# Two attention layers and two feed-forward blocks on one core: GpSimd's five transfers of a round are divided among the round's two steps

## The chip, the cores and the metric

The kernel runs on one core of a Trainium2 chip. The metric is the device time of one execution in microseconds (us); the median of three runs of the kernel before is 3321.29 us (3320.86 to 3324.8). A core has five engines that run side by side, each through its own list of instructions in order: TensorE (PE in the profile), VectorE (DVE), ScalarE (ACT), GpSimd (POOL) and SyncE (SP). Transfers by DMA are issued by SP and by POOL here, and are carried out by the core's 16 DMA engines.

## The reference

The input x has four batches of 1024 rows of 256 numbers, all in 32-bit floats. Four blocks follow one another, each added to x: attention A, a feed-forward block, attention B, and the same feed-forward block again.

```python
x = x + _L0_attn_a_ref(_layernorm(x, axis=-1), L0_attn_a_kernel, L0_attn_a_WO)
x = x + _L0_ffn_ref(_layernorm(x, axis=-1), L0_ffn_w1, L0_ffn_b1, L0_ffn_w2, L0_ffn_b2)
x = x + _L0_attn_b_ref(_layernorm(x, axis=-1), L0_attn_b_w_down_q, ...)
x = x + _L0_ffn_ref(_layernorm(x, axis=-1), L0_ffn_w1, L0_ffn_b1, L0_ffn_w2, L0_ffn_b2)
```

Both attentions have 16 heads of 64 dimensions. For every head the scores of 1024 queries against 1024 keys are put through a softmax and multiplied by the values. Attention B also rotates pairs of dimensions of its queries and keys by the position (the rope).

## The kernel before

An attention works on pairs of heads: 4 batches times 8 pairs, each in 8 **steps** of 128 queries, so 256 steps. Two steps (HB = 2) make a **round**; an attention has 128 of them. One loop, `steps_with`, lists the work of every step for every engine, and each engine keeps that order (the schedule is manual).

For step s the loop asks PE for the scores of step s+1 (L238, into PSUM), DVE for the row maxima (L249), ACT for the exponentials (L251) into a tile p, and DVE for `turn` (L271), a transpose of p in blocks of 32 by 32 into the tile T of the round. The transpose inside 32 by 32 blocks leaves 16 **squares** of 32 partitions by 1088 numbers (136 KB each) that must still go to other partitions. `send` (L288) does that: 16 transfers from T to a second tile, pT. After the second step of a round (an odd s, `part == 0`) SP is given the first 11 squares. In the step after it (an even s, `part == 1`) POOL is given the last five (POOL_DMA = 5). In the loop that call stands before `project`.

Round h of the sends is used later by `weigh(h)` on PE (L297, in step 2h+5), and by `divide(h)` on DVE (L307, the same step), which frees pT. The pools of T and pT have two buffers each. So `turn` of step 2h+4 overwrites T of round h and waits until all 16 transfers of round h have landed, and the transfers of round h+2 wait until `divide(h)` is done.

`project(h)` follows one step after `divide(h)`: PE multiplies with the output weights (L167), ACT copies the product to `got` (L320), and POOL adds it to x (L322).

POOL also issues the loads of weights in attention A (L521, L212, L214). In attention B SP issues those (L629, L212, L214), and POOL has the rope instead. In nearly every round half of a query or key tile is handled: `change` (L645) issues two transfers that swap neighbouring partitions into a tile `turned`, in an odd step; `rotate` (L650 to L652), three elementwise operations, follows at the end of the next, even, step. In some rounds POOL also adds to x a tile that ACT has just normalised (L596), for the next batch.

The lists `pieces` hold such work, by step: those of s - EARLY come between the two halves of the exponentials, those of s at the end of the step.

Of the kernel before, what the change touches and what calls it, by code (L numbers as in the profile page):

```python
# [27 lines left out]
HB = 2  # L28
# [4 lines left out]
POOL_DMA = 5  # L33
# [6 lines left out]
def hybrid_block_kernel(  # L40
# [5 lines left out]
    nc = tc.nc  # L46
# [12 lines left out]
    def group(*shape):  # L59
        last[0] ^= 1  # L60
        return ps_mm.tile([P, *shape], F32, tag=f"m{last[0]}", name="mm")
# [101 lines left out]
    def paired(out, parts, first=True, last=True):  # L163

        for i, (lhsT, rhs) in enumerate(parts):
            for j in range(2):
                nc.tensor.matmul(  # L167
                    out[ts(j, DH)], lhsT[:, ts(j, DH)], rhs[j],
                    start=(first and i == 0), stop=(last and i == len(parts) - 1),
                )  # L170
# [10 lines left out]
    def attention(prep_batch, prep_pair, wo, loader, lead):  # L181
# [22 lines left out]
        n = len(steps)  # L204
# [22 lines left out]
        sc, probs, total, T, pT, av, oT = {}, {}, {}, {}, {}, {}, {}  # L227

        def scores(s):
            g, qs = steps[s]  # L230
            qT, kT = tiles[g]["qT"], tiles[g]["kT"]
            for j in range(2):
                sc[s, j] = ps_sc.tile([P, S], F32, tag="sc", name="sc")
            for m in range(S // 512):
                for half in range(2):
                    for j in range(2):
                        rows = slice(j * DH, (j + 1) * DH)
                        nc.tensor.matmul(  # L238
                            sc[s, j][ts(half, DH), ts(m, 512)],
                            qT()[rows, ts(2 * qs + half, DH)], kT()[rows, ts(m, 512)],  # L240
                            start=True, stop=True,
                        )

        def exponentials(s, j):
            if j == 0:
                probs[s] = pp.tile([P, NK, NG, SQ], F32, tag="p", name="p")
                total[s] = small.tile([P, 2], F32, tag="total", name="total")
            nmax = small.tile([P, 1], F32, tag="nmax", name="nmax")
            nc.vector.tensor_reduce(nmax, sc[s, j], AX.X, ALU.max, negate=True)  # L249
            place = j ^ (s % HB)  # L250
            nc.scalar.activation(  # L251
                probs[s][:, :NK2, ts(j, 2), :],
                sc.pop((s, j)).rearrange("p (k c i) -> p k c i", c=2, i=SQ), AF.Exp,
                bias=nmax, accum_out=total[s][:, place : place + 1],
            )

        def invert(s):
            t = total.pop(s)
            nc.vector.reciprocal(t, t)  # L259
            nc.scalar.copy(  # L260
                probs[s][:, NK2].rearrange("p (j c) i -> p j (c i)", j=2),
                t.unsqueeze(2).to_broadcast([P, 2, DH]),
            )

        def turn(s):
            h, q = divmod(s, HB)
            if q == 0:
                T[h] = tp.tile([P, SENT], F32, tag="T", name="T").rearrange(
                    "p (c q k i) -> p c q k i", c=NG, q=HB, k=NK
                )  # L270
            nc.vector.transpose(  # L271
                T[h][:, :, q, :, :].rearrange("p c k i -> p k c i"), probs.pop(s)
            )
# [3 lines left out]
        squares = [  # L277
            ((a + 2 * i) % NG, (c + 2 * (i ^ x)) % NG)
            for x in range(2) for a in range(2) for c in range(2) for i in range(2)
        ]  # L280

        def send(h, engine, which):
            if h not in pT:
                pT[h] = ptp.tile([P, SENT], F32, tag="pT", name="pT").rearrange(
                    "p (a q k i) -> p a q k i", a=NG, q=HB, k=NK
                )
            for a, c in which:
                engine.dma_start(pT[h][ts(c, SQ), a], T[h][ts(a, SQ), c])  # L288

        def weigh(h):  # L290

            v = tiles[HB * h // NT]["v"]()
            av[h] = [group(P) for q in range(HB)]
            for k in range(NK2):
                for q in range(HB):
                    for j in range(2):
                        nc.tensor.matmul(  # L297
                            av[h][q][ts(j ^ q, DH)], v[ts(j, DH), k, :],
                            pT[h][ts(j, DH), :, q, k, :],
                            start=(k == 0), stop=(k == NK2 - 1),  # L300
                        )

        def divide(h):
            oT[h] = otp.tile([P, HB, P], F32, tag="oT", name="oT")
            R = pT.pop(h)[:, :, :, NK2, :]
            for q, sums in enumerate(av.pop(h)):
                nc.vector.tensor_tensor(  # L307
                    oT[h][:, q].rearrange("p (a i) -> p a i", i=SQ),
                    sums.rearrange("p (a i) -> p a i", i=SQ), R[:, :, q], op=ALU.mult,
                )  # L310

        def project(h):
            g, t0 = divmod(HB * h, NT)
            b, pr = pairs[g]
            po = group(HB, D)
            for t in range(HB):
                paired(po[:, t, :], [(oT[h][:, t], [wos[g][:, t]] * 2)])
            oT.pop(h)
            got = tmp.tile([P, HB, D], F32, tag="tmp", name="got")
            nc.scalar.copy(got, po)  # L320
            xd = xs[b][:, t0 : t0 + HB, :]
            nc.gpsimd.tensor_add(xd, xd, got)  # L322

        def steps_with(others):
            for k, f in others:
                pieces.setdefault(k, []).append(f)
            for s in range(-1, n + LAG + 1):
                h, part = divmod(s - LAG, HB)
                ahead = 0 <= s + 1 < n
                if 0 <= s < n:  # L330
                    invert(s)
                if ahead:
                    scores(s + 1)
                if part == 1 and 0 <= s // HB - 1 < n // HB:
                    send(s // HB - 1, nc.gpsimd, squares[len(squares) - POOL_DMA :])
                    T.pop(s // HB - 1)
                if part == 1 and 0 <= h < n // HB:
                    project(h)
                if ahead:
                    exponentials(s + 1, 0)  # L340
                for f in pieces.get(s - EARLY, ()):
                    f()
                if part == 0 and 0 <= h < n // HB:
                    weigh(h)
                if ahead:
                    exponentials(s + 1, 1)
                if 0 <= s < n:
                    turn(s)
                if part == 0 and 0 <= h < n // HB:
                    divide(h)  # L350
                if part == 0 and 0 <= s < n:
                    send(s // HB, nc.sync, squares[: len(squares) - POOL_DMA])
                for f in pieces.get(s, ()):
                    f()
# [394 lines left out]
```

## Time and profile before

The profiled execution took 3321.26 us; its span, from the first to the last instruction, is 3319.5 us, and some 1.8 us lie around it.

| what | us |
|---|---|
| median of the runs | 3321.29 |
| profiled execution | 3321.26 |
| its span | 3319.5 |
| PE busy, share of the span | 3241.7, 98% |
| DVE | 2626.0, 79% |
| ACT | 1892.7, 57% |
| POOL | 1774.2, 53% |
| attention A, stretch 60 to 1420 us: PE / DVE / POOL busy of 1360 us | 1353.7 / 1246.0 / 578.6 |
| attention B, stretch 1700 to 3066 us: PE / DVE / POOL busy of 1366 us | 1330.3 / 1259.4 / 1084.9 |

In the profile a row of the timeline gives the start, the duration, the engine, the line and the operation; a bracket at its end gives the idle time of the engine just before it and what ended it. "SPq" is SP's queue, which issues transfers; a row that stands for many of them runs from the first issue to the end of the last. The duration of a `DMA_DIRECT2D` row is the time of the issue, not of the transfer; the time to landing is given apart. The busy share of an engine is an average over the whole span, so the table gives the two attentions apart: most of the kernel's time is theirs, and they have different limits.

### The profile page before, as it was taken

Reading aid. Unit: us, or ns where it says so; the run is one execution under the profiler, and the core shown is the slowest. Engines: PE = TensorE matmul, PEld = TensorE weight load, DVE = VectorE, ACT = ScalarE, POOL = GpSimd, SP = SyncE. Lnnn points to the kernel's source line nnn. Section 1 sums busy time; section 2 is a strip of 40 time slices with the busy share of each in tenths; the row PEclk is TensorE's granted clock in tenths of the full one; section 3 lists DMA queues with packets and bytes.
Section 4 is the critical chain, followed back from the end, with each engine's and each line's share of the span. In section 5 each row is a group of like instructions: output and inputs, shape, how many; then the busy total and the mean of one; then the engine's idle time right before and its main releaser. Section 6 shows DMA issues by size and latency. Waiting matters only on the chain.

```text
span 3319.5 us, 124467 instructions
## 1 busy us (share of the span) xinstructions
PE 3241.7 (98%) x52608; PEld 2028.1 (61%) x52608; DVE 2626.0 (79%) x2898; ACT 1892.7 (57%) x3664; POOL 1774.2 (53%) x2482
## 2 busy tenths in 40 slices
PE   8999999999999999999999999999999999998999
PEld 4666666666666666666655655656556656665666
DVE  7998998899988999931069988999899989999100
ACT  5666666665666666643356665666566666665332
POOL 3444444344444444321257887888778878886100
PEclk9999999999999999999999999999999999999999
DMA  8888888888888888830049888998899889998100
GB/s 225 224 218 218 223 224 219 219 220 222 228 212 221 220 225 222 221 82 0 7 126 243 240 241 242 250 248 242 232 247 251 241 235 251 251 254 228 41 20 19
DMA packets 250825, 659.82 MB, mean 199 GB/s; under 512 B 76352, under 2 KB 105024, under 8 KB 250272
## 3 DMA queue, kind: packets, MB, share of 16 engines
q1 hardware_dynamic: 167248, 415.43, 48.0%
q0 software_dynamic: 83024, 236.44, 25.2%
q8 instruction: 418, 6.85, 0.9%
q14 instruction: 135, 1.11, 0.1%
HBM read 43.39 MB, written 4.19 MB: 14 GB/s over the span
## 4 chain that ended last, share of the span: by engine, by line
PE 70%; DVE 9%; SPq 7%; DMA 6%; issue 3%; ACT 3%; POOL 1%; DVEq 0%; ACTq 0%; POOLq 0%
PE sc L238 20%; PE mm L297 18%; PE mm L167 14%; PE mm L413 7%; SPq L288 7%; PE ph L402 6%; DVE T L271 5%; DMA pT<-T 5%; PE mm L176 4%; DVE nmax L249 3%; ACT p L251 1%; PE mm L153 1%; POOL pT L288 1%; DVE oT L307 0%; ACT gT L406 0%
## 5 line engine op out<-in xcount | busy, mean ns | idle before, releaser
L249 DVE TENSOR_REDUCE nmax<-sc 128x1 f32<-128x1024 f32 x1024 | 1202.8, 1216 | 171.1 <-PE sc L238 161.1
L251 ACT ACTIVATE p<-sc,nmax 128x1024 f32<-128x1024 f32 x1024 | 1144.0, 1117 | 329.1 <-DVE nmax L249 328.2
L271 DVE STREAM_TRANSPOSE T<-p 128x2176 f32<-128x2176 f32 x512 | 1246.7, 2435 | 62.2 <-DMA pT<-T 46.8
L288 POOL DMA_DIRECT2D pT<-T x1280 | 625.3, 496 | 1016.8 <-DVE total L259 775.9
L238 PE MATMUL sc<-kT,qT 64*64 64x512 f32 x8192 | 1109.9, 599 | 18.1 <-ACT p L251 15.3
L297 PEld LDWEIGHTS mm<-pT,v 64*64 64x64 f32 x32768 | 960.1, 133 | 159.2 <-issue 105.1
L297 PE MATMUL mm<-pT,v 64*64 64x128 f32 x32768 | 1009.4, 270 | 12.8 <-issue 11.2
L238 PEld LDWEIGHTS sc<-kT,qT 64*64 64x64 f32 x8192 | 347.4, 133 | 408.6 <-issue 276.5
L260 ACT COPY p<-total 128x128 f32<-128x128 f32 x512 | 152.8, 298 | 509.5 <-DVE total L259 503.1
L322 POOL TENSOR_TENSOR x<-x,got 128x512 f32<-128x512 f32 x256 | 330.5, 1291 | 49.4 <-ACT got L320 45.4
L420 DVE TENSOR_TENSOR x<-x,mm 128x512 f32<-128x512 f32 x32 | 21.9, 686 | 364.7 <-PE mm L413 364.7
L167 PE MATMUL mm<-wo,oT 128*64 128x256 f32 x2048 | 277.8, 392 | 13.4 <-DVE oT L307 12.3
L167 PEld LDWEIGHTS mm<-wo,oT 128*64 128x64 f32 x2048 | 124.3, 136 | 260.4 <-DVE oT L307 151.1
L320 ACT COPY got<-mm 128x512 f32<-128x512 f32 x256 | 150.0, 586 | 226.4 <-PE mm L167 225.5
L406 ACT ACTIVATE gT<-ph,b_sb 128x512 f32<-128x512 f32 x128 | 87.5, 686 | 304.3 <-PE ph L402 304.3
L167 PE MATMUL mm<-hT,w 128*64 128x512 f32 x1024 | 243.7, 597 | 1.0 <-ACT hT L156 1.0
L413 PE MATMUL mm<-w_sb,gT 128*128 128x256 f32 x1024 | 226.0, 381 | 6.6 <-ACT hT L156 6.6
L402 PE MATMUL ph<-hT,w_sb 128*128 128x512 f32 x512 | 229.2, 600 | 0.0
L413 PEld LDWEIGHTS mm<-w_sb,gT 128*128 128x128 f32 x1024 | 193.1, 190 | 39.4 <-ACT hT L156 9.4
L251 ACT ACTIVATION_READ_ACCUMULATOR p<-sc,nmax 128x1 f32 x1024 | 204.4, 200 | 0.0
L388 POOL TENSOR_TENSOR x<-x,b_sb 128x256 f32<-128x256 f32 x64 | 44.5, 726 | 275.2 <-ACT xn L147 275.2
L176 PEld LDWEIGHTS mm<-w,hT 128*64 128x64 f32 x4096 | 140.9, 138 | 71.3 <-issue 69.7
(88 smaller groups left out, 2187.5 us busy)
## 6 DMA issues: line engine op xcount, KB each, us to landing
pT<-T SPq DMA_DIRECT2D x2816, 136.0 KB, 4.7
pT<-T POOLq DMA_DIRECT2D x1280, 136.0 KB, 4.6
turned<-kT POOLq DMA_DIRECT2D x128, 128.0 KB, 3.8
turned<-qT POOLq DMA_DIRECT2D x128, 128.0 KB, 3.9
w<-in_wqkv_a POOLq DMA_DIRECT2D x96, 128.0 KB, 6.1
wo<-in_wo_a POOLq DMA_DIRECT2D x32, 128.0 KB, 5.2
wo<-in_wo_a POOLq DMA_DIRECT2D x64, 64.0 KB, 5.6
wo<-in_wo_b SPq DMA_DIRECT2D x32, 128.0 KB, 4.5
```

The costliest lines, as they stand in the source:

```text
L167: nc.tensor.matmul(out[ts(j, DH)], lhsT[:, ts(j, DH)], rhs[j], start=(first and i == 0), stop=(last and i == len(parts) - 1),)
L176: nc.tensor.matmul(out[ts(j, DH)], lhsT, rhs[:, ts(j, DH)], start=(i == 0), stop=(i == len(parts) - 1),)
L238: nc.tensor.matmul(sc[s, j][ts(half, DH), ts(m, 512)], qT()[rows, ts(2 * qs + half, DH)], kT()[rows, ts(m, 512)], start=True, stop=True,)
L249: nc.vector.tensor_reduce(nmax, sc[s, j], AX.X, ALU.max, negate=True)
L251: nc.scalar.activation(probs[s][:, :NK2, ts(j, 2), :], sc.pop((s, j)).rearrange("p (k c i) -> p k c i", c=2, i=SQ), AF.Exp, bias=nmax, acc ...
L260: nc.scalar.copy(probs[s][:, NK2].rearrange("p (j c) i -> p j (c i)", j=2), t.unsqueeze(2).to_broadcast([P, 2, DH]),)
L271: nc.vector.transpose(T[h][:, :, q, :, :].rearrange("p c k i -> p k c i"), probs.pop(s))
L288: engine.dma_start(pT[h][ts(c, SQ), a], T[h][ts(a, SQ), c])
L297: nc.tensor.matmul(av[h][q][ts(j ^ q, DH)], v[ts(j, DH), k, :], pT[h][ts(j, DH), :, q, k, :], start=(k == 0), stop=(k == NK2 - 1),)
L322: nc.gpsimd.tensor_add(xd, xd, got)
L402: nc.tensor.matmul(ph, w1_sb[:, c, ts(f, P)], hT[n][:, c, :], start=(c == 0), stop=(c == NC - 1),)
L413: nc.tensor.matmul(po[n][:, t % 2, :], gT[n][:, f, ts(t, P)], w2_sb[:, f, :], start=(f == 0), stop=(f == NF - 1),)
```

## The change

POOL still issues the same five transfers of every round, in the same order, with the same sources and destinations. Their places in the loop are changed: two before `project` of the even step, one just after it, and the last two in the following odd step, after that step's scores. T is taken out of the table of live tiles there (`T.pop`), one step later than before. The guard in `send` keeps an empty list from making a tile.

```diff
         def send(h, engine, which):
-            if h not in pT:
+            if which and h not in pT:
...
-                if part == 1 and 0 <= s // HB - 1 < n // HB:
-                    send(s // HB - 1, nc.gpsimd, squares[len(squares) - POOL_DMA :])
-                    T.pop(s // HB - 1)
+                g = s // HB - 1
+                others = squares[len(squares) - POOL_DMA :] if 0 <= g < n // HB else []
+                if part == 1:
+                    send(g, nc.gpsimd, others[:2])
                 if part == 1 and 0 <= h < n // HB:
                     project(h)
+                if part == 1:
+                    send(g, nc.gpsimd, others[2:3])
+                if part == 0 and others:
+                    send(g, nc.gpsimd, others[3:])
+                    T.pop(g)
                 if ahead:
                     exponentials(s + 1, 0)
```

The lists of PE, DVE, ACT and SP keep their order. On POOL a round of attention A reads: two sends, the add to x, three sends, then a load where there is one. A round of attention B reads: two sends, the add to x, one send, the three operations of `rotate`, an L596 add in some rounds, two sends, and the two transfers of `change`. Before, all five sends stood ahead of the add.

## The prediction
> **What bounds the kernel now.** The page's busy table would say PE, at 98%. I split it by stage, because the change touches only the two attentions. First the chain of waits in a round of attention A (start, duration, work):
>
> ```profile
> 711.63 0.93 PE mm L176 x32
> 712.56 1.88 PE sc L238 x16
> 714.44 3.49 PE mm L297 x128
> 717.93 1.72 PE sc L238 x16
> ```
>
> With the 2.73 us of L167 these make 10.75 us, a whole round, and nothing but PE is on it. Attention A is bound by PE; a transfer that moves there can only cost, if it comes too late, or do nothing.
>
> Attention B has less PE work, so I read DVE's timeline next:
>
> ```profile
> 2513.44 2.43 DVE L271 STREAM_TRANSPOSE T<-p 128x2176 f32<-128x2176 f32 x1
> 2515.80 0.45 DVE L307 TENSOR_TENSOR oT<-mm,pT 128x128 f32<-128x128 f32 x2
> ...
> 2519.00 2.44 DVE L271 STREAM_TRANSPOSE T<-p 128x2176 f32<-128x2176 f32 x1
> ...
> 2530.21 2.44 DVE L271 STREAM_TRANSPOSE T<-p 128x2176 f32<-128x2176 f32 x1 [1.01 <-DMA pT<-T]
> ```
>
> A round has four maxima of 1.18 us (pairs of 2.36), two transposes of 2.43, two L307 in 0.45 and two reciprocals of 0.13: 10.3 us. The transposes of B start between 1692.2 and 3066.8 us, 127.5 rounds, so a round takes 10.78 us on average. DVE is nearly the bound there, and a DVE stall is paid in full or nearly. The last row shows such a stall: the transpose was due at 2529.20 and waited for round h's transfers. DVE's waits from 1690 to 3070 us:
>
> ```profile
> DVE nmax L249 <- PE sc L238: 51.3, 71, 3.0
> DVE T L271 <- DMA pT<-T: 38.7, 29, 3.2
> ```
>
> With 3.8 us put down to w and wo loads (7 times), 42.5 us in 36 stalls are waits of `turn` for landings. In A the same wait is 8.0 us in 20 pieces, and PE covers it. So 42.5 us is what this change can win at most, and the wait that it can lengthen.
>
> Which transfers end these stalls? SP's queue, same stall (its round's second transpose ended at 2515.87):
>
> ```profile
> 2515.59 1.16 SPq L214 DMA_DIRECT2D wo<-in_wo_b  x2
> 2516.99 17.83 SPq L288 DMA_DIRECT2D pT<-T  x22
> ```
>
> SP was late by the wo loads and then took 0.81 us a send, against 0.51 for its shortest: its queue is held back. The eleventh send starts near 2516.99 + 10 x 0.81 = 2525.1 and, at the 4.3 us median landing of this stretch, lands near 2529.4. POOL's five were issued from 2516.54 to 2518.97 and land by 2526.2 even at the longest landing of a POOL send (7.2 us). **SP's tail decides, and POOL's transfers are over 3 us early.** SP's queue waits for DVE 64 times in this stretch, 342.8 us, 257.7 of them in one feed-forward block: 85 us in 1366, so it is occupied 94% of the time.
>
> **The change part by part.** All five POOL sends cost 0.49 us of POOL each, before and after; none is added. What moves is read from POOL's round (transpose ended at 2505.32):
>
> ```profile
> 2506.00 2.43 POOL L288 DMA_DIRECT2D pT<-T  x5 [0.89 <-DMA pT<-T]
> 2508.45 1.29 POOL L322 TENSOR_TENSOR x<-x,got 128x512 f32<-128x512 f32 x1
> 2509.69 1.28 POOL L650 TENSOR_TENSOR qT<-qT,cos_sb 128x512 f32<-128x512 f32 x1
> ...
> 2512.27 1.28 POOL L652 TENSOR_TENSOR qT<-qT,turned 128x512 f32<-128x512 f32 x1
> 2513.84 1.13 POOL L645 DMA_DIRECT2D turned<-kT  x2 [0.30 <-POOL qT L652]
> 2516.54 2.43 POOL L288 DMA_DIRECT2D pT<-T  x5 [1.56 <-DVE total L259]
> ```
>
> *Two sends, then the add.* Two sends end at 2506.98. The add now waits for `got`, which ACT finishes at 2507.44 + 0.59 = 2508.03: a new wait of 1.1 us on POOL, with the third send and `rotate` behind it. The add runs from 2508.1 to 2509.4, the third send to 2509.9, so `rotate` starts 0.2 us later than before. That costs nothing: it was the five sends that filled this time.
>
> *The last two sends* go behind `rotate`, to 2513.7 and 2514.2, 8.4 and 8.9 us after the transpose instead of 2.2 and 2.6. `change` follows at 2514.7 instead of 2513.84, ends at 2515.9, and POOL is free 0.6 us before its next sends (2516.54). Its two transfers took 3.9 to 4.2 us to land here, so the second lands near 2519.5; `rotate` of the next round started at 2520.23. Spare before 1.7 us, after 0.7. I charge 1 us in all for rounds where that is used up.
>
> *Do the last two land in time?* T is needed 13.7 us after the transpose (2519.00 - 2505.32), in the stalled round 13.3. The fifth send, at 8.9, may take 4.4 to 4.8 us. The trace has no POOL send of T in this phase, so I bound it. The Trainium skill, "DMA: Bandwidth & Descriptors", section "Anatomy of one DMA — SWDGE (gpsimd) path", prices a GpSimd transfer at about 2.0 us plus bytes / 436e3: for 139,264 bytes 2.3 us, my estimate from it. The trace's shortest is also 2.3, but its median is 4.7, because others are in flight. The nearest row is `change` in the same phase, with its 3.9 to 4.2 us for 128 KB. By the page the send lands at 11.2, over 2 us early; by the row at 12.8 to 13.1, 0.2 to 0.9 us early; by the median at 13.6, on the edge. I take the row, 4.0 us: in time, but no longer with ample cover.
>
> *An L596 add* stands ahead of the last two sends in 12 of B's rounds (24 adds, half of them after `change`). At 0.736 us each the fifth send goes to 9.6 and lands at 13.6: about 0.3 us late, 12 x 0.3 = 4 us.
>
> *What SP gains.* In windows of this round the DMA engines move (window, length, busy of PE, PEld, DVE, ACT and POOL, clock, DMA share, GB/s):
>
> ```profile
> 2508.80:2510.80 2.00, 2.00 (x32) 1.03 (x28) 2.00 (x1) 2.00 (x6) 2.00 (x2) 1.00 0.94 283
> 2510.80:2512.80 2.00, 2.00 (x64) 1.73 (x62) 1.94 (x4) 1.01 (x3) 1.92 (x3) 1.00 0.89 311
> 2514.80:2515.90 1.10, 1.10 (x17) 0.79 (x12) 1.10 (x2) 0.00 (x0) 0.18 (x1) 1.00 0.91 217
> ```
>
> Two transfers, 279 KB, leave the crowded middle for the emptier end. At 283 to 311 GB/s that is 0.90 to 0.98 us less ahead of SP's tail. The rule against it is the skill's, same page, section "Issuing engines are not separate DMA queues": whoever issues them, all transfers share the same 16 engines, and issuing from several engines only saves the sequencer's time. By that rule alone the bytes of a round are the same and nothing moves: 0. By the rows the order within the round decides, since `turn` waits for the last landing and POOL's sat 3 us early. Ends: 0 and 0.98 us a stall; I take 0.55. Over 36 stalls (mean 1.18 us) that is **20 us**.
>
> *Attention A.* `got` ends 2.2 us after the transpose (710.60 against 708.4), the three late sends follow each other from 3.6 to 5.0 us, and land by 9.6 at the 4.6 us median; T is needed at 13.6 or later. The w loads behind them slip from 712.87 to 713.5, a landing of 6.1 us with three steps in hand. Cost 0.
>
> *Ends of the attentions.* The very last round's third send waits for `got` until 1439.7 instead of 1429.7, and the last two wait behind four L388 adds until 1443.7; the fifth lands by 1448.8, and `weigh` starts at 1451.41. In B it is 3085.2, 3090.3 and 3092.95. Cost 0; cover 2.6 us.
>
> Sum: -20 + 4 + 1 = -15 us. The profiled execution took 3321.26 us (span 3319.5), the median is 3321.29: the two agree, and the forecast is **3306 us**.
>
> **The rivals.**
> 1. *Forecast*: SP's tail shortens, POOL's last two fit. 3290 to 3314. Chance 0.48.
> 2. *Nothing moves*: the bytes decide. For it: B's DMA share of 0.90 and SP's 94% leave little air; against it, the 217 GB/s at a round's end. 0 + 5 = about 3321, up to 3326. Chance 0.18.
> 3. *The last two sends become the last landing*, with `change` queued behind them. The mechanism is one place: POOL, behind `rotate`; it decides once such a send takes over 4.8 us to land (the median is 4.7, POOL's sends reach 7.2). At 5.5 us T is 0.7 to 1.1 us late; a late round puts back the deadline of the next, so about every second of 126 rounds pays: 63 x 0.9 = 57 us, less the 20 won: 3358. At 5.0 us, 63 x 0.4 - 20 = +5: 3326. For it: POOL's spare time falls to 0.6 us a round. Chance 0.27.
> 4. *All stalls of `turn` in B vanish*: 3321 - 42 = 3279. Chance 0.07.
>
> **How the numbers follow.** The time is rival 1's. The range 3282 to 3346 takes in rival 2, most of rival 3 and the edge of 4; about 2 in 10 lie outside. Rival 1's own range is 3290 to 3314. A difference under 0.2% (6.6 us) can't be told from none. Faster: most of 1 and all of 4, 0.52; within 0.2%: 2 with the rims of 1 and 3, 0.19; slower: 0.29.
>
> **What would show it.** Right: the wait of `turn` for pT in B falls from 38.7 to some 20 us, SP takes less than 0.8 us a send, attention A's rounds stay at 10.75. Wrong by rival 3: that wait grows, and POOL shows waits of L650 for `turned` (2.7 us in three pieces for kT now). Wrong by rival 2: SP's pace and the wait stay.

## The result, and the profile after

The changed kernel took 3334.44 us, median of 10 runs (3327.87 to 3337.33), against 3324.8 us for 10 runs of the kernel before on the same chip (3319.0 to 3329.5). The ratio is 1.0027, 95% interval 1.0019 to 1.0036: it is slower, by some 9 us (0.27%; the medians differ by 9.6). The forecast was 3306 us and faster; the time lies in its range, the sign is wrong. The profiled execution took 3332.81 us, its span is 3331.0 us, 11.5 more than before.

Where are the 11.5 us? An attention is taken from the start of its first transpose (L271) to the end of its last, both read from DVE's timeline:

| stretch | before | after | difference |
|---|---|---|---|
| attention A | 1397.7 | 1400.7 | +3.0 |
| between | 264.1 | 264.6 | +0.5 |
| attention B | 1377.1 | 1384.6 | +7.5 |
| start and end together | 280.6 | 281.1 | +0.5 |

In this execution both attentions lost, and nothing else did. But one execution is not the median: among the experiments below, the profiles with an untouched A have 1395.2 to 1398.5 us for A, those with an untouched B 1374.9 to 1380.7 us for B. The medians of the experiments part the 9 us otherwise.

Two waits of the kernel before in attention B, and then those of the kernel after (1690 to 3085 us; who waited for whom, sum in us, times, longest):

```profile
POOL kT L650 <- DMA turned<-kT: 2.7, 3, 1.6
POOL qT L650 <- DMA turned<-qT: 0.5, 1, 0.5
```

```profile
POOL x L322 <- ACT got L320: 60.7, 103, 1.3
DVE T L271 <- DMA pT<-T: 42.9, 26, 3.4
DVE nmax L249 <- PE sc L238: 40.0, 57, 3.0
POOL kT L656 <- DMA turned<-kT: 34.4, 33, 2.7
POOL qT L656 <- DMA turned<-qT: 21.0, 27, 2.1
```

Four things are to be seen. The wait of `turn` that is put down to landings of pT grew from 38.7 to 42.9 us; it was to fall to about 20. The trace often names another event as the releaser; over all releasers the wait of `turn` went from 50.3 to 71.9 us. `rotate` (L650 before, L656 now) waits 55.4 us for `turned`, where it waited 3.2 us. The add waits for `got`, 0.6 us each time; the forecast had 1.1 us, at no cost. And DVE's waits for PE's scores fell, from 51.3 to 40.0 us. I take this for part of a stall of `turn` that comes back: PE gets ahead while DVE stands.

The transfers of the whole kernel by issuer (size, median us to landing), before and after:

```profile
pT<-T SPq DMA_DIRECT2D x2816, 136.0 KB, 4.7
pT<-T POOLq DMA_DIRECT2D x1280, 136.0 KB, 4.6
turned<-kT POOLq DMA_DIRECT2D x128, 128.0 KB, 3.8
turned<-qT POOLq DMA_DIRECT2D x128, 128.0 KB, 3.9
```

```profile
pT<-T SPq DMA_DIRECT2D x2816, 136.0 KB, 4.5
pT<-T POOLq DMA_DIRECT2D x1280, 136.0 KB, 4.2
turned<-kT POOLq DMA_DIRECT2D x128, 128.0 KB, 4.3
turned<-qT POOLq DMA_DIRECT2D x128, 128.0 KB, 4.2
```

The squares land a little sooner, `change`'s transfers 0.3 to 0.5 us later.

One stalled round of B in the kernel after, POOL's timeline and then DVE's (start, duration, work; in brackets the idle time before and what ended it). The round's second transpose ended at 2021.37:

```profile
2022.04 1.00 POOL L288 DMA_DIRECT2D pT<-T  x2 [1.51 <-DVE total L259]
2023.61 1.27 POOL L322 TENSOR_TENSOR x<-x,got 128x512 f32<-128x512 f32 x1 [0.57 <-ACT got L320]
2024.83 0.53 POOL L288 DMA_DIRECT2D pT<-T  x1
2026.77 1.26 POOL L656 TENSOR_TENSOR qT<-qT,cos_sb 128x512 f32<-128x512 f32 x1 [1.42 <-DMA turned<-qT]
...
2030.58 1.04 POOL L288 DMA_DIRECT2D pT<-T  x2
```

```profile
2018.94 2.43 DVE L271 STREAM_TRANSPOSE T<-p 128x2176 f32<-128x2176 f32 x1
...
2036.15 2.44 DVE L271 STREAM_TRANSPOSE T<-p 128x2176 f32<-128x2176 f32 x1 [1.56 <-DMA pT<-T]
```

`rotate` wanted to start at 2025.35 and waited 1.42 us for the two transfers that `change` had issued from 2019.4 on; they took 6.0 and 6.6 us to land. So the last two sends went out 9.2 and 9.8 us after the transpose; the forecast had 8.4 and 8.9. Their way to landing:

```profile
DMA to landing us min/median/max: 3.0/3.8/4.5
```

The later one landed at 2035.7. T was due at 2034.59. SP's last, issued at 2030.4, had landed at 2033.7: **the last landing had passed from SP to POOL**, as rival 3 had it.

That can be counted. The first transpose of a round overwrites the T of two rounds earlier. For every stall of such a transpose in B (over 0.05 us) the landings of that T's 16 transfers say which came last:

| B of | ended by SP's landing: stalls, us | by POOL's |
|---|---|---|
| before | 44, 45.9 | 0 |
| after | 27, 37.5 | 38, 30.4 |

### The profile page after: what moved, and what is told of

The parts are those of the page before. It is cut to its first block, busy times and chain, and to the rows that moved or that the text cites. A ratio compares the mean times of both kernels' runs of the same rounds, so it can differ in the third digit from the quotient of the medians.

```text
span 3331.0 us, 124467 instructions
## 1 busy us (share of the span) xinstructions
PE 3245.8 (97%) x52608; PEld 2022.0 (61%) x52608; DVE 2623.1 (79%) x2898; ACT 1893.7 (57%) x3664; POOL 1772.5 (53%) x2482
## 4 chain that ended last, share of the span: by engine, by line
PE 64%; DVE 10%; DMA 9%; SPq 7%; issue 5%; ACT 3%; POOL 2%; DVEq 0%; POOLq 0%; ACTq 0%
PE sc L238 18%; PE mm L297 15%; PE mm L167 14%; PE mm L419 7%; SPq L288 7%; PE ph L408 6%; DMA pT<-T 6%; DVE T L271 5%; PE mm L176 4%; DVE nmax L249 3%; DMA turned<-kT 1%; ACT p L251 1%; DMA turned<-qT 1%; DMA wo<-in_wo_b 1%; POOL turned L657 1%
## 5 line engine op out<-in xcount | busy, mean ns | idle before, releaser
L271 DVE STREAM_TRANSPOSE T<-p 128x2176 f32<-128x2176 f32 x512 | 1247.2, 2436 | 95.4 <-DMA pT<-T 59.5
L249 DVE TENSOR_REDUCE nmax<-sc 128x1 f32<-128x1024 f32 x1024 | 1202.3, 1215 | 150.2 <-PE sc L238 140.9
L288 POOL DMA_DIRECT2D pT<-T x1280 | 645.3, 507 | 875.5 <-DVE total L259 741.1
```

What stands on the lines that cost most here:

```text
L271: nc.vector.transpose(T[h][:, :, q, :, :].rearrange("p c k i -> p k c i"), probs.pop(s))
```

## The experiments

All edits use one form of the loop; only the pair (`first`, `second`) is chosen anew. `loader` is POOL in attention A alone. Before it is (5, 5), after (2, 3).

```diff
+                if part == 1:
+                    send(g, nc.gpsimd, others[:first])
                 if part == 1 and 0 <= h < n // HB:
                     project(h)
+                if part == 1:
+                    send(g, nc.gpsimd, others[first:second])
+                if part == 0 and others:
+                    send(g, nc.gpsimd, others[second:])
+                    T.pop(g)
```

All ratios are to the kernel before on the same chip, with 95% intervals. The runs of one kernel spread over 7 to 24 us, so a difference is taken from medians, and single profiles serve only to see where it lies.

### Which attention?

**a_only**: the change in A alone.

```diff
+                first, second = (2, 3) if loader is nc.gpsimd else (5, 5)
```

> The change in attention A alone (two sends, add, three sends); B as before. Theory 'late' (the loss is B's last two sends, which stand behind rotate and become the last landing of a round): A has no rotate, so the time is that of before, within 3 us, and the wait of turn for pT in A stays near 8 us. Theory 'crowded tail' (the sends that wait for got meet SP's last sends on the DMA engines, in both attentions): +4 to +6 us, the wait of turn in A rises to some 18 us as in the changed kernel, and SP's last sends of a round take over 0.8 us each.

Measured: 1.0017 (1.0008 to 1.0026), 3329.68 against 3323.52 us: +6 us from the part that was to cost nothing. (The profiled execution, 3319.14 us, is the fastest of its 22, so this loss can't be read from it.)

**b_only**: the change in B alone.

```diff
+                first, second = (5, 5) if loader is nc.gpsimd else (2, 3)
```

> The change in attention B alone; A as before. 'Late': the whole loss, +8 to +11 us, wait of turn for pT in B 55 us or more. 'Crowded tail': about half of it, +4 to +6 us.

Measured: 1.0001 (0.9992 to 1.0010): no difference. Both parts together make +6, the change +9; that fits within the intervals. So most of the loss is attention A's, and B's forecast gain is missing.

**after_add**: nothing behind `rotate`; three sends after the add, in both attentions.

```diff
+                first, second = (2, 5)
```

> Two sends, add, then the other three sends at once, in both attentions: A as in the changed kernel, but in B nothing stands behind rotate. 'Late': B returns to before or better, so the time is that of before within 3 us (or up to 10 us below, if SP's tail gains from the three that left the front). 'Crowded tail': A keeps its +4 to +6 us and B has the same cost as A, +8 to +12 us in all.

Measured: 0.9997 (0.9988 to 1.0006). On POOL, A's order is the same as in a_only, so B should have won what A lost. The profile agrees, with A at 1407.0 us and B at 1374.0 (before 1397.7 and 1377.1); b_add3 below tests it.

**six**: the order of before, but SP gives one square to POOL, in both attentions.

```diff
-POOL_DMA = 5
+POOL_DMA = 6
...
+                first, second = (6, 6)
```

> The order of before (all of POOL's sends ahead of the add), but six squares by POOL and ten by SP. If SP's tail is what ends the rounds of before, one send of 0.8 us less on SP takes 0.5 to 0.8 us off most of the 36 stalls in B: -10 to -25 us. If only the bytes of a round count: within 3 us of before. If POOL's own time in B is short (half a us more a round ahead of rotate): slower, with waits of rotate for turned.

Measured: 1.0002 (0.9992 to 1.0012). A shorter list on SP is worth nothing here, with the sixth send added at the crowded front: in B SP's last landing is no earlier, 12.9 us after the transpose as a median (12.8 before).

### Attention B: what is won, and what takes it back?

**b_add3**: two sends in front of the add and three behind it, in B alone.

```diff
+                first, second = (5, 5) if loader is nc.gpsimd else (2, 5)
```

> Attention A as before; in B two sends, add, three sends, and none behind rotate. If the parts add up (the changed A costs some 6 us, the changed B nothing, and this B has -7 us in it): -4 to -9 us. If the differences between the runs so far are only scatter: within 3 us of before.

Measured: 0.9975 (0.9963 to 0.9986), 3313.77 against 3322.79 us. It beats both kernels by more than the 0.2% (6.6 us) that the prediction took for the least difference. Its waits in B:

```profile
POOL x L322 <- ACT got L320: 83.6, 107, 9.7
DVE nmax L249 <- PE sc L238: 43.2, 63, 3.0
DVE T L271 <- DMA pT<-T: 30.0, 27, 3.0
...
POOL kT L657 <- DMA turned<-kT: 2.8, 3, 1.7
```

POOL waits 83.6 us for `got` and it costs nothing; `rotate` hardly waits. Over all releasers `turn`'s wait is the same as before (50.1 to 50.3 us). What fell is DVE's wait for scores, by 8.1 us. Single profiles scatter: the five with B untouched have 47.8 to 54.8 us for the first, 46.3 to 51.3 for the second, 98.3 to 103.3 for the sum. The sum of b_add3, 93.3, lies below all of them. The gain is real, but no shorter wait of `turn` is to be seen in it.

**b_late3**: three sends behind `rotate`.

```diff
+                first, second = (5, 5) if loader is nc.gpsimd else (2, 2)
```

> A as before; in B two sends, add, rotate, and then three sends instead of two behind rotate. 'Late' (sends behind rotate are the last landing in B): the fifth goes out half a us later than in the changed kernel, the wait of turn for landings in B rises above the changed kernel's, +10 to +25 us. If SP's tail still decides: 0 or below, since one more transfer has left its front.

Measured: 1.0104 (1.0086 to 1.0121), +34 us, more than the dearest expectation.

**b_after_change**: the last two sends stand behind `change`, at the end of the odd step, so that `change` isn't delayed.

```diff
+                first, second = (5, 5) if loader is nc.gpsimd else (2, 3)
...
                     f()
+                if part == 0 and others:
+                    send(g, nc.gpsimd, others[second:])
+                    T.pop(g)
```

> A as before; in B two sends, add, one send, rotate, the two transfers of change, and only then the last two sends (0.8 to 1 us later than in the changed kernel). Theory 'loop' (in B the two sends delay change, rotate of the next round waits for its landing, and the sends behind rotate go out later still): without sends between rotate and change the rope's waits fall from some 53 us back under 10, and the time is that of B alone or below, -9 to 0 us. Theory 'late sends' (only the lateness of the two sends counts): still later sends, +8 to +25 us over before, with the rope's waits small.

Measured: 1.0149 (1.0135 to 1.0163), +51 us. Its waits in B:

```profile
DVE T L271 <- DMA pT<-T: 69.6, 36, 4.1
...
DVE nmax L249 <- PE sc L238: 28.6, 36, 3.0
...
POOL kT L657 <- DMA turned<-kT: 2.5, 3, 1.8
```

`rotate`'s wait is gone, 2.5 us, and the kernel is much slower. So the delay of `change` is not what costs in itself; the lateness of the last sends is.

**b_35**: three in front of the add, two behind.

```diff
+                first, second = (5, 5) if loader is nc.gpsimd else (3, 5)
```

> A as before; in B three sends, add, two sends, none behind rotate: between before (five, add) and the run with two, add, three (-9 us). If the gain grows with what leaves the front: -3 to -7 us. If any division ahead of rotate gives it: -7 to -10 us.

Measured: 0.9984 (0.9976 to 0.9992), -5 us: it stands between before and b_add3.

**b_add4**: b_add3 with a sixth square for POOL, ten for SP, in B alone.

```diff
+        mine = POOL_DMA if loader is nc.gpsimd else POOL_DMA + 1
...
+                others = squares[len(squares) - mine :] if 0 <= g < n // HB else []
+                first, second = (5, 5) if loader is nc.gpsimd else (2, 6)
...
-                    send(s // HB, nc.sync, squares[: len(squares) - POOL_DMA])
+                    send(s // HB, nc.sync, squares[: len(squares) - mine])
```

> A as before; in B six squares by POOL, as two, add, four; ten by SP. If SP's tail in B is still what ends the late rounds: below the -9 us of two, add, three, -12 to -20 us. If POOL's half us more a round ahead of rotate makes the rope wait: above it, -5 to +10 us, with the rope's waits over 15 us.

Measured: 0.9973 (0.9963 to 0.9983), 3313.86 us. It equals b_add3; the further gain is missing.

One table over B's profiles. The places are the numbers of sends ahead of the add, behind it, and behind `rotate`; the stalls are counted as above; T is the wait of `turn` over all its releasers, nmax that of L249 for PE; B is the length of the attention; the last column is the difference of medians to before. In the profiles of b_add4 and b_after_change one landing record is missing, and the landings of one SP transfer in eight are worked out from the neighbouring records.

| kernel | places | stalls by SP, us | by POOL, us | T | nmax | B, us | time |
|---|---|---|---|---|---|---|---|
| before | 5/0/0 | 44, 45.9 | 0 | 50.3 | 51.3 | 1377.1 | |
| b_35 | 3/2/0 | 56, 45.4 | 0 | 49.5 | 44.8 | 1371.3 | -5 |
| b_add3 | 2/3/0 | 54, 46.1 | 0 | 50.1 | 43.2 | 1369.5 | -9 |
| b_add4 | 2/4/0 | 62, 41.4 | 2, 1.3 | 46.6 | 45.5 | 1369.7 | -10 |
| b_only | 2/1/2 | 25, 28.2 | 46, 33.9 | 66.3 | 39.5 | 1377.4 | 0 |
| b_late3 | 2/0/3 | 13, 14.4 | 71, 85.2 | 104.1 | 37.0 | 1410.8 | +34 |
| b_after_change | 2/1/2 at the step's end | 5, 7.8 | 79, 120.9 | 132.8 | 28.6 | 1430.2 | +51 |

The later POOL's last sends go, the fewer stalls are SP's and the more are POOL's. T and nmax together move by -7.3, -8.3, -9.5, +4.2, +39.5 and +59.8 us, down the table: that is the time within some 5 us, and within 9 in the last row.

### Attention A: why does it cost at all?

**a_w**: the change in A in every fourth round only, those with a load of w behind POOL's sends.

```diff
+                first, second = (2, 3) if loader is nc.gpsimd and g % 4 == 1 else (5, 5)
```

> B as before; in A the change is made only in the rounds in which POOL also loads w (every fourth). Theory 'loads' (the loss in A comes where three late sends and three loads follow each other on POOL and meet SP's tail): the whole loss of A, +4 to +8 us, with single waits of turn of 1.5 us and more in these rounds. Theory 'every round' (SP's tail is later everywhere): a quarter of it, +1 to +2 us.

Measured: 1.0007 (0.9998 to 1.0017).

**a_rest**: the change in A in all the other rounds.

```diff
+                first, second = (2, 3) if loader is nc.gpsimd and g % 4 != 1 else (5, 5)
```

> B as before; in A the change in all rounds but those with w loads. 'Loads': within 2 us of before, no wait of turn over 1.2 us in A after the first rounds. 'Every round': three quarters of the loss, +4 to +5 us.

Measured: 1.0016 (1.0010 to 1.0023), +5.5 us. So the loads are not the main cost: the 96 rounds without them lose 0.16%. For the 32 with loads the interval takes in zero. The profile tempts to another story. In the longest stall of `turn` in A of the kernel after, 2.32 us at 724.32, SP's last three squares of the round that it waited for look like this (issue in ns, first and last start; then min, median and max us to landing):

```profile
L288 SPq DMA_DIRECT2D pT<-T x3: 592/593/603, 715.0 to 716.3; - x3
...
DMA to landing us min/median/max: 7.0/7.8/7.8
```

In front of them POOL had issued its three late sends and three loads of w (711.86 to 715.54). It is a load round, and such rounds have most of the stalls, but not most of the cost.

**a_all_after**: all five behind the add, in A alone.

```diff
+                first, second = (0, 5) if loader is nc.gpsimd else (5, 5)
```

> B as before; in A all five sends behind the add that waits for got (none ahead of it), so two more transfers meet SP's last ones. 'Crowded tail': the loss in A grows beyond the +6 us of the split, +8 to +20 us, with more waits of turn in A than the 17 us of that kernel. If the loss in A has another cause (the place of the add, or scatter): +6 us or less.

Measured: 1.0026 (1.0017 to 1.0036), 3333.13 us against 3323.8: +9 us. Its waits in A:

```profile
POOL x L322 <- ACT got L320: 784.6, 123, 8.9
...
DVE T L271 <- DMA pT<-T: 31.5, 31, 2.8
```

Before, these two rows of A had 1.2 us in 4 waits and 8.0 us in 20. All 42 stalls of a first transpose in A, 42.3 us, ended with a landing of SP. POOL's squares, though issued later than before, are in time in every one of them. Over A's 128 rounds SP's last landing moved, as a median, from 12.36 us after the transpose (before) to 12.64 (after) and 13.19 (a_all_after), its 95th percentile from 13.8 to 14.2 and 15.1; in all three all but one round in twenty want T no earlier than 13.4. So the late POOL sends are not late themselves: they make SP's tail late.

How much of A's cost comes this way is another question. The stalls of a first transpose in A, all ended by SP, and how much of them waited for a load round:

| kernel | rounds changed | stalls, us | of these, for load rounds | A, us | time |
|---|---|---|---|---|---|
| before | none | 23, 9.3 | 8.4 | 1397.7 | |
| a_w | the 32 with loads | 23, 16.4 | 14.9 | 1401.3 | +0.5 |
| a_rest | the 96 others | 20, 9.9 | 7.1 | 1401.8 | +5.5 |
| a_only | all | 27, 15.1 | 10.0 | 1396.1 | +6 |
| a_all_after | all, five behind the add | 42, 42.3 | 30.5 | 1411.0 | +9 |

The lengths of A are of single executions. a_w stalls 7 us longer than before at a cost that can't be told from none; a_rest stalls as before and takes 5.5 us more. So the stalls of `turn` don't account for A's loss. They grew most for the load rounds, which cost little; how the other rounds lose is not shown.

## Why the prediction was wrong

Point by point, by its own steps:

The forecast was -15 us and some +9 were measured. Of these 24 us A makes 6 (a_only), B 15 (b_only: 0 where -15 was forecast), and 3 lie within the intervals.

- **Attention A's "Cost 0" failed**, and is where time was lost: it measured +6 us. The step asked whether POOL's three sends would be in time, and they were: in the kernel after they are issued 3.5 to 4.5 us after the transpose and the last has landed by 10.0 in the median round, where the forecast had 3.6 to 5.0 and 9.6. It didn't ask what they meet. SP's last send is issued earlier than before (7.94 against 8.41 us after the transpose, medians), but takes 4.58 instead of 4.02 us to land (means). The sum lacked the same reasoning by bytes that it used for B, with the other sign. "A transfer that moves there can only cost, if it comes too late" named only half of it: it can also make another late. That PE bounds A held in the middle: the median round is 10.75 us in both kernels, but the 95th percentile went from 11.7 to 12.3. By which wait the 6 us reach the time stays open (a_rest).

- **"SP's tail decides" held; "What SP gains" was right in the median and too large in the stalls.** All 44 stalls counted in B before end with SP. SP's last landing in B moved from 12.82 to 12.29 us (b_only, medians), 0.53 against 0.55 forecast, and its step from send to send fell from 0.81 to 0.76 us, below the 0.8 named as a sign. The stalls that SP ends fell from 45.9 to 28.2 us in b_only and to 37.5 in after, against -20. But part of this fall is a change of name: POOL now ends stalls in which SP was late too. The time by which SP's last landing missed the moment when T was due, summed over all rounds, was 29.4 us before, 18.1 in b_only and 27.3 in after; in the five profiles with B untouched it is 24.1 to 30.3. So SP won some 11 us at best, and a gain in the late rounds is not firmly shown.

- **"I take the row, 4.0 us: in time" failed, though every number in it was good.** In b_only the last two sends were issued at 8.4 and 9.0 us on average (forecast 8.4 and 8.9) and took 3.7 and 4.1 us. Their last landing has a median of 13.05 us, in the forecast 12.8 to 13.1. But a quarter of the rounds land after 13.9, and T is due at 13.3 to 13.7 by the forecast; measured, it is due at 13.55 in the median round, and before 12.7 in one of twenty. One typical landing was set against one typical deadline; the spread of both was left out, and it made 46 stalls of 33.9 us. `turn` as a whole waits 16 us longer than before, and B, forecast at -15, measured 0. With none behind `rotate` (b_add3) POOL ends no stall and B gains 9. The price of the Trainium skill ("DMA: Bandwidth & Descriptors", section "Anatomy of one DMA — SWDGE (gpsimd) path"), 2.3 us by the prediction's estimate from it, was 1.8 short of the 4.1 measured for the fifth send; the row was 0.1 short.

- **The L596 term (4 us) came about as forecast.** In the profile of after POOL ended stalls in 5 of these 12 rounds, 4.6 us.

- **"I charge 1 us in all" for `change` was mis-sized as a wait**: `rotate` waits 52.7 us in b_only and 55.4 in after, and its transfers land 0.3 to 0.5 us later than before (3.8 and 3.9 us before; in after 4.3 and 4.2). In the stalled round above the wait pushed the last sends back; as a cost of its own it is not shown: without it (b_after_change) the kernel loses 51 us, and the last sends are later still, at 9.6 and 10.1 us on average.

- **"A DVE stall is paid in full or nearly" was off.** In b_only T rose by 16.0 us, and nmax fell by 11.8, as if PE got ahead while DVE stood. In b_late3 T rose by 53.8 us, and 34 were paid.

- **Rival 3** named the place and the mechanism, for B. Its price, +37 us (57 less 20), was set for more and longer stalls than came, 63 x 0.9 against 46 x 0.74, all of them paid in full. No rival had A's loss.

- **Rival 2's rule**, the skill's ("DMA: Bandwidth & Descriptors", section "Issuing engines are not separate DMA queues"), was rightly set aside as a bound of zero: the same transfers by the same engines gave from -9 to +51 us by their place in the round. The lateness of SP's squares in A fits its first half, that transfers run on the same engines and interleave, whoever issued them.

What stays open: how A loses 5.5 us in rounds in which `turn` doesn't stall longer (a_rest); and which waits of PE b_add3 spares. Its T is unchanged and nmax falls; the table shows that the two add up to the gain, not why it falls there. Nor is it shown why a tenth square for SP instead of eleven is worth nothing, at the front (six) or behind the add (b_add4).

## What to carry to other kernels

When a transfer is moved out of a crowded moment, ask two questions: whether it still lands in time at the late end of its landing times, not the middle, and whose transfers it will meet where it goes. A transfer with much to spare is best moved only as far as the crowd ends: here behind one add (-9 us), not behind the next block of work (0), and in attention A, where SP's last landing was in time only just, not at all (+6 us). Count, for each stall, which of the transfers it waits for landed last; the sum of a wait says nothing of who ends it.

## What was not expected of the hardware

Transfers of `change` that took 3.8 and 3.9 us in the median before took 4.3 and 4.2 after, though they left POOL only some 0.6 us later in B's round (9.1 us after the transpose against 8.5, medians); in the stalled round above single ones, right behind two squares, took 6.0 and 6.6 us. And in A SP's tail was slower to land although SP issued it earlier, when POOL's three transfers came in the middle of its list: SP's steps from its eighth send to the ninth and on to the tenth grew to 1.05 and 0.72 us (medians), from 0.64 each, while the steps from the fifth to the sixth and seventh, where they had been before, shrank from 1.22 and 1.08 to 0.81 and 0.64.
